# Gated graph network and graph attention, 32 pairs of graphs on one core: the candidate's two products as one operation, the last pair's W product ahead of its softmax, and new leads

## Chip, core and metric

One core of one Trainium2 chip. The metric is the device time of one execution in microseconds, as the median of several runs; the kernel before has 1939.04 us over 3 runs (1937.46 to 1940.88). The profile is of one further execution, whose own time is 1938.19 us.

## What is computed

`x` holds 64 graphs of 256 nodes with 256 features, `adj` their 0/1 edges. All is f32.

```
# layer 0
h = max(layernorm(x), 0)
for i in range(3):
    aggr = A^T (h weight[i])                 # A = (adj != 0)
    gi, gh = aggr w_ih^T + b_ih, h w_hh^T + b_hh
    r, z = sigmoid(i_r + h_r), sigmoid(i_z + h_z)
    n = tanh(i_n + r * h_n)                  # the candidate state
    h = (1 - z) * n + z * h
x = x + h
# layer 1
h = max(layernorm(x), 0);  v = h W^T
e = leaky_relu(v a_left [:, None] + v a_right [None, :])
alpha = softmax(where(adj, e, -1e9))
x = x + alpha v
```

## The kernel before

Graphs go two by two: 32 pairs, and a tile [128, 512] holds one half (`db`) of the features of all 512 nodes of a pair, or for node-major data one graph. TensorE computes in parts: an f32 operand is rounded to f32r (`v0`), and two f16 tiles carry what is left (`v1`) and a copy (`vd`). A product of such operands is one f32r pass (j = 0) and two f16 passes (j = 1, 2) per block of 128 inputs. `split16` (L695) makes the three tiles with two or three instructions of ACT and DVE.

`setup` (L536) turns and splits the weights. It also multiplies `weight[i]` with w_ih^T into one matrix G_i (L657 to L669), so that the aggregate of h itself meets G_i in place of the two products. ACT rounds and copies here (`three`, L644 to L651, `factor`, L600). TensorE starts with 12 transposes of the identity that nobody reads (`fill`, L540, L545); two and five more stand ahead of two later transposes (L546, L626).

`pair(p)` (L812) makes the operations of one pair. Per layer i, `prop` (L862) multiplies h by the adjacency; `split16` splits h (`hs`) and the aggregate (`gs`). Then, per half db of the features, `gate` (L737) makes the products: r with w_hh ahead and with G_i behind, as two operations into one bank ("topT" and "topF"); `nh`, the candidate's product with w_hh (L894), followed by an ACT instruction that adds the bias (L756); `ni`, its product with G_i (L899), in a bank of its own; and z with both (L903). DVE forms (1 + r) * nh (L897), adds ni (L900), ACT takes the tanh (L902) and that of z (L905), and DVE combines (L909 to L913). `passes` (L731) lists the six matmuls of one matrix, and an operation sorts its passes by j:

```python
            seq = [q for m, s in terms for q in passes(bank, cols, m, ts(e, P), s, first)]
            seq.sort(key=lambda q: ((1, 2, 0) if narrow[0] else (0, 1, 2)).index(q[0]))
```

`narrow` tells whether the operation before ended on f16 passes; then this one begins with them and ends on f32r. So each operation changes once between f32r and f16. After the three layers come the residual (L932, L951), the norm, the attention scores, exponentials and two products per graph: `mix` (softmax with h) and `project` (the result with W^T). All pairs but the last turn h and the softmax by DMA (`dma_turn`, L760) and join the halves on ACT (L779).

The last pair has nothing behind it. From its second layer on its two graphs go one by one (`apart`, L853), with 256 columns per matmul, and its attention goes by blocks of 128 rows (L1078 to L1112): exponentials, a transpose by TensorE, a copy, `mix` of 4 products of 128 columns (L1095), a copy (L1102), `project` of 2 products of 256 columns (L1104), the update (L1109) and the store.

The order on each engine is a planner's (`Plan`, L231). `op` notes engine, modelled cost and tiles; `run` (L311) places, again and again, the operation that can start first, ties going to the lower `prio`. That is a due time passed back from its readers, less a lead by name from the table `LEAD` (L28). An operation waits for the earlier operations on its tiles and for a free buffer of its class; there are 8 accumulator banks. `in_turn` (L284) keeps the gate products of one turn (pair and layer, `TURN`, L1117) behind those of the turn before, so that two pairs alternate. Engines run what they get in that order.

Of the kernel before, what the change touches and what calls it, by code (L numbers as in the profile page):

```python
# [25 lines left out]
SWITCH = 16  # L26
SAME = {"PE": 0, "ACT": 115, "DVE": 115, "POOL": 0}
# [3 lines left out]
    "A": -447500, "G 0": 29000, "G 1": -7000, "G 2": 49000, "b_rz": 117000, "b_rz half": -29000, "back 0": -1500,  # L31
    "back 0 gather": 26000, "back 0 of 0": 15000, "back 1": -85000, "back 1 of 0": -54500, "back 1 of 1": 30500,
    "back copy 0": -202500, "back copy 1": 105000, "c0 0": -60000, "c0 1": 76500, "c0 d": -91500, "c1 0": 10500,
    "c1 1": -78500, "c1 d": -12500, "d add 0 of 0": -4000, "d add 1": 65500, "d add 1 of 0": 36500,
    "d add 1 of 1": -5000, "d mul 0": 7500, "d mul 0 of 0": 19500, "d mul 1": 4000, "d mul 1 of 0": 1000,
    "d mul 1 of 1": 44500, "d sub 0": -8500, "d sub 0 of 0": 4000, "d sub 0 of 1": 69000, "d sub 1": 210000,
    "d sub 1 of 0": -169500, "d sub 1 of 1": -32500, "dot 0": -56000, "dot 1": -80000, "exps 0": -5000,
    "exps 0 1": 11500, "exps 1": -24000, "exps 1 0": 500, "fill": 4000, "first A": -28000, "first A16": -2500,
    "first back 0": -8000, "first back 0 gather": -35000, "first back 1": 101500, "first c0 0": -4000,
    "first c0 1": 24500, "first c0 d": 50000, "first c1 0": -8500, "first c1 1": -133500, "first c1 d": 27500,  # L40
    "first d add 0": 5000, "first d add 1": 23000, "first d mul 0": 35500, "first d sub 0": -38000,
    "first d sub 1": 33000, "first dot 0": 4500, "first dot 1": -4000, "first exps 0": 18000, "first exps 1": 41000,
    "first fill": -500, "first g0 0": 39000, "first g0 1": -17000, "first g1 0": 1000, "first g1 1": 8000,
    "first g1 d": -52000, "first h0 0": 8500, "first h0 1": -36500, "first h0 d": 2000, "first h1 0": -30500,
    "first h1 1": 72000, "first h1 d": -8000, "first hi 1": 46000, "first in 0 eps": -36500, "first in 0 pow": -12500,
    "first in 0 relu": 10500, "first in 0 shift": 6000, "first in 0 stats": -60000, "first in 1 eps": -28500,
    "first in 1 pow": -44500, "first in 1 relu": 79000, "first in 1 shift": -19500, "first in 1 stats": -2000,
    "first in hi 0": 125500, "first in hi 1": 39500, "first in lo 0": 51500, "first in lo 1": 500,
    "first leaky 0": 45000, "first leaky 1": -15000, "first line 0": -28500, "first line 1": -46000,
    "first lo 0": -7000, "first lo 1": 13000, "first load": -47500, "first m0 0": 48000, "first m0 1": -10500,  # L50
    "first m0 d": -47500, "first m1 0": 44000, "first m1 1": 72500, "first m1 d": -10000, "first max 0": -13500,
    "first max 1": 8000, "first mid 0 eps": -30500, "first mid 0 pow": 44500, "first mid 0 relu": -33000,
    "first mid 0 shift": -19500, "first mid 0 stats": 20000, "first mid 1 eps": 15000, "first mid 1 pow": 69000,
    "first mid 1 relu": 70500, "first mid 1 shift": -26500, "first mix 0": -50000, "first mix 1": -29000,
    "first nh 0 scale": -20000, "first nh 1 scale": 10000, "first nh 1 topF": 53000, "first ni 0 topF": -6500,
    "first ni 1 topF": -54000, "first out 0": 62000, "first out 1": -500, "first p copy 0": -31500,
    "first p copy 1": -18000, "first p turn 0": -54500, "first p turn 0 gather": 31500, "first p turn 1 gather": 3000,
    "first p0 1": 55000, "first p1 0": -29000, "first p1 1": -16500, "first p1 d": 80500, "first project 0": -22000,
    "first project 1": -7500, "first prop 0": 6000, "first prop 1": -6000, "first r 0": 3000,
    "first r 0 topF": -17000, "first r 1": 51500, "first r 1 topF": 55500, "first r 1 topT": -177500,  # L60
    "first res 0": 47000, "first res 1": -500, "first right 0": -4500, "first right 1": -14000, "first store": 2500,
    "first tanh 0": -59500, "first tanh 1": -3000, "first total": -2000, "first turn 0": -6000, "first turn 1": 40500,
    "first turn copy 0": 500, "first turn copy 1": 44000, "first u 0": 16500, "first u 1": 1500,
    "first u add 0": 16000, "first u add 1": 9500, "first w load full": 4000, "first z 0": -29500,
    "first z 0 topF": -36500, "first z 1 topF": 17500, "g0 0": -9000, "g0 0 of 0": 16000, "g0 0 of 1": -31000,
    "g0 1": -8500, "g0 1 of 0": 16000, "g0 1 of 1": 111000, "g0 d": -25500, "g0 d of 0": 57500, "g0 d of 1": -45500,
    "g1 0": 28000, "g1 0 of 0": -193500, "g1 0 of 1": 1000, "g1 1": 500, "g1 1 of 0": -32000, "g1 1 of 1": 2000,
    "g1 d": 193500, "g1 d of 0": 23500, "g1 d of 1": -5500, "h0 0": -4000, "h0 0 of 0": -115000, "h0 0 of 1": -38000,
    "h0 1": -77000, "h0 1 of 0": -25500, "h0 1 of 1": -12000, "h0 d": -77500, "h0 d of 0": 21500, "h0 d of 1": -28000,
    "h1 0": -72500, "h1 1": -241000, "h1 1 of 0": 87000, "h1 1 of 1": 15500, "h1 d": -212500, "h1 d of 0": -5500,  # L70
    "h1 d of 1": -43000, "hi 0": 23500, "hi 0 of 0": -4000, "hi 0 of 1": 66000, "hi 1": -46000, "hi 1 of 0": -17000,
    "hi 1 of 1": -23000, "ident": -44000, "in 0 eps": 6000, "in 0 pow": -8000, "in 0 shift": -134000,
    "in 0 stats": -10000, "in 1 eps": 4500, "in 1 pow": -8000, "in 1 relu": -2500, "in 1 shift": -307500,
    "in 1 stats": -74500, "in hi 0": -250500, "in hi 1": -91500, "in lo 0": -37500, "last A": 5500, "last A16": 60000,
    "last back 0": 20500, "last back 0 of 0": 4000, "last back 0 of 1": -30000, "last back 1": -99000,
    "last back 1 of 0": -68500, "last d add 0": -33500, "last d add 0 of 0": -154500, "last d add 0 of 1": -33000,
    "last d add 1": 2500, "last d add 1 of 0": 27000, "last d add 1 of 1": -4500, "last d mul 0": -133000,
    "last d mul 0 of 0": -161500, "last d mul 0 of 1": -16000, "last d mul 1 of 0": 5500, "last d mul 1 of 1": -15500,
    "last d sub 0 of 0": -32500, "last d sub 0 of 1": -22500, "last d sub 1": -8000, "last d sub 1 of 0": 24500,
    "last d sub 1 of 1": -125000, "last dot 0": -12000, "last dot 1": 2000, "last exps 0 1": 5000,  # L80
    "last exps 1 0": 10000, "last exps 1 1": 74000, "last fill": 32500, "last g0 0": -97000, "last g0 0 of 0": 97000,
    "last g0 0 of 1": 32000, "last g0 1": 52000, "last g0 1 of 0": 45000, "last g0 1 of 1": -3500,
    "last g0 d": -31000, "last g0 d of 0": -127500, "last g0 d of 1": 5000, "last g1 0": -2000,
    "last g1 0 of 0": -4000, "last g1 1": -11000, "last g1 1 of 0": 102000, "last g1 1 of 1": -18000,
    "last g1 d": 4000, "last g1 d of 0": 161000, "last g1 d of 1": -63500, "last h0 0 of 0": 96000,
    "last h0 0 of 1": 60000, "last h0 1": -66000, "last h0 1 of 0": 35500, "last h0 1 of 1": 19500, "last h0 d": -500,
    "last h0 d of 0": 48000, "last h0 d of 1": -19500, "last h1 0": -1000, "last h1 0 of 0": 37000,
    "last h1 0 of 1": 6500, "last h1 1": 10000, "last h1 1 of 0": 29500, "last h1 1 of 1": 10000, "last h1 d": 20000,
    "last h1 d of 0": 84000, "last h1 d of 1": -10000, "last hi 0": 27500, "last hi 0 of 0": 16000,
    "last hi 0 of 1": -14500, "last hi 1": 4000, "last hi 1 of 0": 33000, "last hi 1 of 1": -2000,  # L90
    "last in 0 eps": 2000, "last in 0 pow": 500, "last in 0 relu": 30000, "last in 0 shift": 57000,
    "last in 0 stats": -18500, "last in 1 eps": 81000, "last in 1 pow": -24000, "last in 1 relu": 16500,
    "last in 1 stats": -32000, "last in hi 0": 81500, "last in hi 1": 16000, "last in lo 0": 15000,
    "last in lo 1": -40500, "last leaky 0": 25000, "last leaky 1": 18000, "last lo 0": 27000,
# [289 lines left out]
def tile_gated_gnn_then_gat(  # L384
# [40 lines left out]
    P = 128  # L425
# [727 lines left out]
```

## Time and profile before

| | |
|---|---|
| median of 3 runs | 1939.04 us |
| profiled execution, own time | 1938.19 us |
| its span | 1936.4 us |
| TensorE busy | 1926.1 us, 10320 matmuls |
| VectorE (DVE) busy | 1647.3 us |
| ScalarE (ACT) busy | 1599.8 us |
| GpSimd (POOL) busy | 197.1 us |
| granted TensorE clock | 1.00 |

The span runs from the first to the last recorded instruction, or the landing of what it stored. A row of the timeline names start and length in us, engine (PE is TensorE, PEld its weight loads), line, operation, written and read tiles, shapes and how many instructions it merges; "f32" with `round` tiles is f32r. In brackets is the engine's idle time before it and what ended it. A matmul's end is modelled, so the distance of two starts tells more than a length. The chain goes back from the last instruction to what released each step.

### The profile page before, as it was taken

The page shows a single profiled execution, that of the slowest core. Times are in us where ns is not written, and L with a number is a line of the kernel's source. Part 1 is how long each engine was busy: PE and PEld are TensorE (multiplying, and loading weights), DVE is VectorE, ACT ScalarE, POOL GpSimd, SP SyncE. Part 2 cuts the span into 40 slices and gives each one's busy share as a digit, 9 for nine tenths or more (in the row PEclk, how much of TensorE's full clock was granted, in tenths as well). Part 3 has the DMA queues.
Part 4 walks back from the last instruction along what each step waited for, and adds up shares of the span by engine and source line. Part 5 has one row for each costly group of instructions (what it writes and reads, how often), then busy time and mean ns, then how long its engine had stood idle before and what let it go on. Part 6 is the DMA issues. An engine that isn't in the chain of part 4 may idle for free.

```text
span 1936.4 us, 31621 instructions
## 1 busy us (share of the span) xinstructions
PE 1926.1 (99%) x10320; PEld 1214.5 (63%) x10320; DVE 1647.3 (85%) x3951; ACT 1599.8 (83%) x2801; POOL 197.1 (10%) x280
## 2 busy tenths in 40 slices
PE   9999999999999999999999999999999999999999
PEld 6556665666666666656666656666566666566667
DVE  7678888888888888889888888888888888888887
ACT  7668888888888888888888888889888888888876
POOL 3001111001011001010010110010110101100000
PEclk9999999999999999999999999999999999999999
DMA  5157786667776777866677877678766777667642
GB/s 142 36 113 125 136 139 126 122 121 151 133 123 119 132 130 141 135 124 119 123 149 132 123 128 124 129 145 136 121 120 124 144 137 122 136 113 128 118 82 61
DMA packets 738119, 240.24 MB, mean 124 GB/s; under 512 B 662160, under 2 KB 737952, under 8 KB 737952
## 3 DMA queue, kind: packets, MB, share of 16 engines
q1 hardware_dynamic: 737920, 238.20, 67.5%
q8 instruction: 81, 1.33, 0.3%
q14 instruction: 86, 0.70, 0.2%
q10 hardware_dynamic: 32, 0.01, 0.0%
HBM read 60.83 MB, written 16.84 MB: 40 GB/s over the span
## 4 chain that ended last, share of the span: by engine, by line
PE 91%; ACT 3%; DMA 2%; DVE 2%; SPq 1%; issue 1%; POOL 0%; ACTq 0%; POOLq 0%
PE bank L734 73%; PE bank L873 8%; PE bank L1056 4%; PE bank L1037 4%; DMA full<-full 2%; SPq L771 1%; ACT full L779 1%; PE bank L664 1%; ACT round L702 0%; ACT half L707 0%; DVE half L704 0%; ACT round L720 0%; DVE small L794 0%; ACT full L807 0%; PE bank L1098 0%
## 5 line engine op out<-in xcount | busy, mean ns | idle before, releaser
L734 PE MATMUL bank<-half,low_hh 128*128 128x512 f16 (+1 forms) x2352 | 613.8, 376 | 0.0
L734 PE MATMUL bank<-half,low 128*128 128x512 f16 (+1 forms) x2352 | 611.7, 375 | 0.1
L734 PE MATMUL bank<-round,fac_hh 128*128 128x512 f32 (+1 forms) x1176 | 411.6, 437 | 0.0
L734 PE MATMUL bank<-round,fac 128*128 128x512 f32 (+1 forms) x1176 | 395.0, 425 | 0.0
L734 PEld LDWEIGHTS <-low 128*128 128x128 f16 x2352 | 216.3, 98 | 267.4 <-issue 45.3
L734 PEld LDWEIGHTS <-low_hh 128*128 128x128 f16 x2352 | 206.2, 98 | 265.3 <-issue 78.9
L779 ACT COPY full<-full 128x1024 uint16<-128x1024 uint16 x306 | 355.7, 1174 | 15.4 <-DMA full<-full 15.2
L734 PEld LDWEIGHTS bank<-round,fac 128*128 128x128 f32 x1176 | 218.6, 189 | 61.5
L734 PEld LDWEIGHTS bank<-round,fac_hh 128*128 128x128 f32 x1176 | 217.1, 189 | 62.7
L801 POOL TENSOR_TENSOR small<-small,nhalf 128x2 f32<-128x2 f32 x128 | 114.5, 902 | 1268.4 <-DVE small L799 1199.3
L704 DVE SCALAR_TENSOR_TENSOR half<-bank,round 128x512 f16<-128x512 f32 (+1 forms) x254 | 171.3, 683 | 48.8 <-ACT half L707 30.8
L756 ACT ACTIVATE bank<-bank,b_nh 128x512 f32<-128x512 f32 (+1 forms) x196 | 127.1, 650 | 96.2 <-PE bank L734 95.9
L905 ACT ACTIVATE full<-bank,b_rz 128x512 f32<-128x512 f32 (+1 forms) x196 | 132.6, 676 | 86.0 <-PE bank L734 85.3
L892 ACT ACTIVATE full<-bank,b_rz 128x512 f32<-128x512 f32 (+1 forms) x196 | 133.8, 683 | 60.4 <-PE bank L734 60.1
L704 DVE SCALAR_TENSOR_TENSOR half<-full,round 128x512 f16<-128x512 f32 (+1 forms) x254 | 170.2, 679 | 8.9 <-ACT round L702 6.1
L702 ACT ACTIVATE round<-bank 128x512 fp32r<-128x512 f32 (+1 forms) x254 | 152.0, 599 | 15.0 <-PE bank L873 11.3
L702 ACT ACTIVATE round<-full 128x512 fp32r<-128x512 f32 (+1 forms) x254 | 155.9, 642 | 6.4 <-DVE full L913 5.2
L721 DVE SCALAR_TENSOR_TENSOR half<-full,round 128x512 f16<-128x512 f32 x184 | 125.9, 686 | 41.1 <-ACT round L720 36.4
L902 ACT ACTIVATE full<-full,vec 128x512 f32<-128x512 f32 (+1 forms) x196 | 140.4, 717 | 24.2 <-DVE full L900 24.2
L911 DVE SCALAR_TENSOR_TENSOR full<-full,full 128x512 f32<-128x512 f32 (+1 forms) x196 | 130.8, 678 | 32.8 <-ACT full L905 32.4
L909 DVE TENSOR_TENSOR full<-full,full 128x512 f32<-128x512 f32 (+1 forms) x196 | 132.8, 678 | 24.6 <-ACT full L902 24.5
L707 ACT ACTIVATE half<-bank 128x512 f16<-128x512 f32 (+1 forms) x254 | 142.6, 601 | 3.7 <-PE bank L873 3.1
(120 smaller groups left out, 2526.2 us busy)
## 6 DMA issues: line engine op xcount, KB each, us to landing
full<-full SPq DMA_DIRECT2D x488, 128.0 KB, 3.5
x<-in_x_dram SPq DMA_DIRECT2D x64, 256.0 KB, 3.2
adj<-in_adj_dram SPq DMA_DIRECT2D x64, 256.0 KB, 3.4
full<-in_x_dram SPq DMA_DIRECT2D x64, 256.0 KB, 3.3
full<-full SPq DMA_DIRECT2D x248, 64.0 KB, 2.5
out_dram<-full SPq DMA_DIRECT2D x62, 256.0 KB, 2.9
full<-line SPq DMA_DIRECT2D x60, 128.0 KB, 4.1
full<-full SPq DMA_TRANSPOSE x306, 3.3
```

What stands on the lines that cost most here:

```text
L702: act(f"{name} 0{of}", cut(A512 if bank else C512), lambda: nc.scalar.activation(v0.t[:, cols], v.t[:, cols], AF.Copy, scale=up), r=[(v, h ...
L704: dve_(f"{name} 1{of}", cut(V512), lambda: nc.vector.scalar_tensor_tensor(v1.t[:, cols], v.t[:, cols], up, v0.t[:, cols].bitcast(F32), op0 ...
L707: act(f"{name} d{of}", cut(A512), lambda: nc.scalar.activation(vd.t[:, cols], v.t[:, cols], AF.Copy, scale=up * unit), r=[(v, has)], w=[(v ...
L734: return [(j, lambda start, j=j, kb=kb: nc.tensor.matmul(bank.t[:, cols], fs(j, kb), s[kb][j].t[:, cols], start=start, stop=True, skip_gro ...
L756: act(name + " scale", fit(575, part), lambda: nc.scalar.activation(bank.t[:, cols], bank.t[:, cols], AF.Identity, bias=bias), r=[("b_nh", ...
L779: act(name, 1065, lambda: nc.scalar.copy(dst.t.bitcast(U16).rearrange("p (j n b) -> p j n b", j=2, b=2), src.t.bitcast(U16).rearrange(f"p ...
L873: nc.tensor.matmul(pa.t[:, ts(g, N)], b, m[:, ts(sb, N)], start=(n == 0), stop=True, skip_group_check=True)
L892: act(f"r {db}{of}", fit(575, part), lambda b=r_, k=pr, db=db, cols=cols: nc.scalar.activation(b.t[:, cols], k.t[:, cols], AF.Tanh, bias=b ...
L902: act(f"tanh {db}{of}", fit(615, part), lambda u=u, en=en, cols=cols: nc.scalar.activation(u.t[:, cols], u.t[:, cols], AF.Tanh, bias=b_i[: ...
L905: act(f"z {db}{of}", fit(575, part), lambda b=z_, k=pz, db=db, cols=cols: nc.scalar.activation(b.t[:, cols], k.t[:, cols], AF.Tanh, bias=b ...
L909: dve2(f"d sub {db}{of}", fit(V512, part), lambda u=u, d=d, cols=cols: nc.vector.tensor_sub(d.t[:, cols], d.t[:, cols], u.t[:, cols]), r=[ ...
L911: dve2(f"d mul {db}{of}", fit(V512, part), lambda d=d, b=z_, cols=cols: nc.vector.scalar_tensor_tensor(d.t[:, cols], b.t[:, cols], 1.0, d. ...
```

## The change

1. `nh` and `ni` become one operation, `new_state`, of 12 matmuls into two banks, sorted by j over both. It replaces the calls at L894 and L899; the ACT and DVE instructions behind them stay. It can start when both the split h and the split aggregate are there, and w_hh and G_i.
2. In the last pair, `h` of each graph is turned by TensorE once its norm is there, copied, multiplied by W^T and copied (`hW`). `mix` is then 2 products of 256 columns per block with `hW`, and its result goes to the update directly. The copy at L1102 and `project` at L1104 go.
3. In `setup`, 11 idle transposes in place of 12 at the start, and in place of the two fixed groups the planner asks for idle transposes in the gaps that it models on TensorE before 12.5 us (all of a gap before 6.5 us, 0.6 of it after, none below one transpose's time). For kb = 1 of w_ih and of `weight[0]` the f16 copy is DVE's in place of ACT's: three instructions.
4. The first loads are modelled at 3200 ns in place of 3900.
5. `LEAD` is replaced: of the names in both tables 4 keep their value.

```diff
+HEAD, COLD, TURN_COLD, TURN_WARM = 12500.0, 6500.0, 213.0, 109.0
...
+            if o.eng == "PE" and self.idle is not None and t < HEAD:
+                gap, slow = t - pe_free, t < COLD
+                if gap > TURN_COLD and pe_free > 0.0:
+                    self.idle(int(gap / TURN_COLD) if slow else int(0.6 * gap / TURN_WARM))
+                s = max(pe_free, t)
+                pe_free = s + (2 * o.occ if slow and o.name != "warm" else o.occ)
...
-        plan.op(name, "SP", 1000, 3900, fn, **kw)
+        plan.op(name, "SP", 1000, 3200, fn, **kw)
...
-        pe("warm", 2500, lambda: fill(12), r=[("ident", ONE)], w=[(idle, ONE)])
-        between = {"0": 2, "1": 5}
+        pe("warm", 2500, warm, r=[("ident", ONE)], w=[(idle, ONE)])
+        plan.idle = fill
...
-            act(f"w d {tag}", 100 + 0.75 * n, lambda: nc.scalar.activation(put(vd), b.t[:, :n], AF.Copy, scale=up), r=[(b, ONE)], w=[(vd, ONE)])
+            if tag in ("ih", 0) and kb == 1:
+                dve(f"w d {tag}", 75 + 1.04 * n, lambda: nc.vector.tensor_scalar(put(vd), b.t[:, :n], up, None, op0=ALU.mult), r=[(b, ONE)], w=[(vd, ONE)])
+            else:
+                act(f"w d {tag}", 100 + 0.75 * n, lambda: nc.scalar.activation(put(vd), b.t[:, :n], AF.Copy, scale=up), r=[(b, ONE)], w=[(vd, ONE)])
...
+    def new_state(name, e, hs, i, gs, tops, bias, part=ALL):
+
+        ph, pn = Buf("bank"), Buf("bank")
+        cols, cost, cost16 = columns(part), PASS if len(part) == 2 else PROP, PASS16 if len(part) == 2 else PROP16
+
+        def go():
+            seq = [(j, bank, run) for bank, m, s in ((ph, "hh", hs), (pn, i, gs)) for j, run in passes(bank, cols, m, ts(e, P), s, True)]
+            started = set()
+            for j, bank, run in sorted(seq, key=lambda q: ((1, 2, 0) if narrow[0] else (0, 1, 2)).index(q[0])):
+                run(bank not in started)
+                started.add(bank)
+
+        tops.append(pe(name + " topF", 4 * (cost + 2 * cost16), go, mixed=True, w=[(ph, ONE), (pn, ONE)],
...
+        act(name + " scale", fit(575, part), lambda: nc.scalar.activation(
+            ph.t[:, cols], ph.t[:, cols], AF.Identity, bias=bias), r=[("b_nh", ONE)], w=[(ph, ONE)])
+        return ph, pn
...
-                    ph = gate(f"nh {db}{of}", en, [("hh", hs)], tops, bias=b_nh[:, db : db + 1], part=part)
+                    ph, pn = new_state(f"nh {db}{of}", en, hs, i, gs, tops, b_nh[:, db : db + 1], part=part)
...
-                    pn = gate(f"ni {db}{of}", en, [(i, gs)], tops, part=part)
...
+        hW = [Buf("full") for _ in range(G)]
+        for g in range(0 if far else G):
...
+            pe(f"h turn {g}", 4 * TR, turn_h, r=[(hb[g], ALL), ("ident", ONE)], w=[(tb, ONE)])
+            act(f"h copy {g}", A512, lambda tb=tb, ht=ht: nc.scalar.copy(ht.t, tb.t), r=[(tb, ONE)], w=[(ht, ONE)])
...
+                        nc.tensor.matmul(pw.t[:, ts(jb, D)], ht.t[:, db * N + jb * P : db * N + (jb + 1) * P], wT[:, db, :],
+                                         start=(db == 0), stop=(db == DB - 1))
+
+            pe(f"hW {g}", 4 * MM, project_rows, r=[(ht, ONE), ("wT", ALL)], w=[(pw, ONE)])
+            act(f"hW copy {g}", A512, lambda pw=pw, b=hW[g]: nc.scalar.copy(b.t, pw.t), r=[(pw, ONE)], w=[(hW[g], ONE)])
...
-            act("mix copy" + name, fit(A512, ONE), lambda ag=ag, pg=pg: nc.scalar.copy(ag.t[:, :N], pg.t[:, :N]), r=[(pg, ONE)], w=[(ag, ONE)])
...
-            pe("project" + name, 2 * MM, project, r=[(ag, ONE), ("wT", ALL)], w=[(pv, ONE)])
+            def mix(g=g, pT=pT, pv=pv):
+                for jb in range(NB):
+                    nc.tensor.matmul(pv.t[:, :D], pT.t[:, ts(jb, P)], parts(hW[g])[:, jb, :], start=(jb == 0), stop=(jb == NB - 1))
+
+            pe("mix" + name, 2 * MM, mix, r=[(pT, ONE), (hW[g], ONE)], w=[(pv, ONE)])
```

## The prediction

> **What bounds the kernel now.** I read the page's busy times and its chain first, then windows of time, then the chain in order of time, and last the timeline of both ends.
>
> ```profile
> span 1936.4 us, 31621 instructions
> ...
> PE 1926.1 (99%) x10320; PEld 1214.5 (63%) x10320; DVE 1647.3 (85%) x3951; ACT 1599.8 (83%) x2801; POOL 197.1 (10%) x280
> ...
> PE 91%; ACT 3%; DMA 2%; DVE 2%; SPq 1%; issue 1%; POOL 0%; ACTq 0%; POOLq 0%
> ```
>
> TensorE is busy in 1926.1 of 1936.4 us and is 91% of the chain. Only 10.3 us can be idle; the next table says where.
>
> ```profile
> 0.00:10.00 10.00, 7.38 (x42) 6.36 (x42) 4.10 (x18) 5.88 (x14) 3.50 (x12) 1.00 0.81 247
> ...
> 400.00:1000.00 600.00, 600.00 (x3191) 375.87 (x3190) 519.83 (x1236) 507.42 (x877) 59.97 (x82) 1.00 0.71 131
> ...
> 1700.00:1800.00 100.00, 97.85 (x521) 60.47 (x519) 86.14 (x207) 81.91 (x142) 9.02 (x12) 1.00 0.66 118
> ...
> 1912.00:1937.00 25.00, 19.82 (x120) 16.46 (x119) 14.40 (x50) 13.34 (x32) 0.95 (x2) 1.00 0.13 44
> ```
>
> Columns are the window, its length, then busy time and count of PE, PEld, DVE, ACT and POOL, then the granted clock. PE idles 2.6 us in the first 10, nothing in the middle, 2.15 in the hundred before 1800, and about 4.6 behind 1912 (the span ends at 1936.4). The chain in order of time repeats with the pair:
>
> ```profile
> 342.06 2.71 PE bank L1037 x24
> ...
> 401.08 2.71 PE bank L1037 x24
> ```
>
> One pair costs 59.02 us, all of it matmuls without a hole. So in the middle only less PE work, or cheaper PE work, shortens the kernel; an earlier DVE or ACT result does nothing there. Elsewhere it is the two ends.
>
> **Merging the candidate state's products** (L894 and L899 become one operation). The matmuls are the same: 6 + 6 before, 12 after. What goes is a change between f32r and f16 passes, which each operation makes once. Price from the 128x512 matmuls of L734, start to start: f16 to f16 is 216 ns, f32 to f32 inside a run 233, f32 to f16 232; from the last f16 to the second f32 it is 451 (216 + 233 would be 449), and the first f16 behind an f32 takes 226. There and back cost 2 + 10 = 12 ns. By whole runs it is less: four f32 in a row cost 945 ns up to the steady f16, six cost 1415; the step is 235 each and leaves 5. The page counts 196 instructions of L756, so 196 operations go and with them 98 changes there and back: 98 times 5 to 12 ns, **0.5 to 1.2 us; I take 0.8**.
>
> The operation now alternates between two accumulators. The row: sixteen f16 matmuls in a row belong to two operations with two banks, and stay at 216 ns with the clock at 1.00. "TensorE: Matmul & The Clock Gate" in the Trainium skill (section "A second HAM failure mode: psum-queue depth-cycling") says that going round the banks can let the clock fall back and forth. It gives no price that I can put in the sum; the row says nothing is lost, and I go by the row.
>
> What the merger takes away is freedom. The h products (L894) need no aggregate and run while ACT and DVE still split it; the candidate's aggregate products (L899) need no w_hh. Three places use that.
>
> In the middle (494 to 497 us) the h products of r and of the candidate lie around the propagation. There the other pair's z products, two operations of 2.7 us, can stand in; ACT and DVE have 15% to spare. I cost it at nothing; if the cover were gone it would be the 1.35 us of one candidate operation per layer, and the period would show it at once.
>
> In the last pair, graphs go apart and cover is thin:
>
> ```profile
> 1906.13 0.60 PE L734 MATMUL bank<-half,low_hh 128*128 128x256 f16 x4
> ...
> 1907.06 0.61 PE L734 MATMUL bank<-half,low_hh 128*128 128x256 f16 x4
> 1907.51 0.38 PE L873 MATMUL bank<-half,half 128*128 128x256 bf16 x2
> ...
> 1908.10 0.48 PE L734 MATMUL bank<-round,fac_hh 128*128 128x256 f32 x2
> ...
> 1909.01 0.48 PE L734 MATMUL bank<-round,fac 128*128 128x256 f32 x2
> 1909.33 1.05 PE L734 MATMUL bank<-half,low 128*128 128x256 f16 x8
> ```
>
> and, in the same timeline, the split that they wait for:
>
> ```profile
> 1908.85 0.42 DVE L704 SCALAR_TENSOR_TENSOR half<-bank,round 128x256 f16<-128x256 f32 x1 [0.36 <-ACT half L707]
> ```
>
> The split of the last aggregate ends on DVE at 1909.27, and the f16 products that read it start at 1909.33: no slack. Until then PE lives on products with w_hh, four operations of six matmuls from 1904.99 on, some 0.68 us each. Two of them (1.36 us) are the candidate's and must now wait. The last propagation (1907.51) needs ACT's rounding of 1905.63, which stood behind the previous pair's exponentials; ordered before them it could run up to 1 us earlier and win back most of this. Bounds 0 and +1.36; **I take +0.7**, the middle. The other such places of the last pair (eight candidate operations in all, 5.4 us) still have the previous pairs' attention products beside them, and I cost them at nothing.
>
> At the start the aggregate half of the candidate fills PE twice (22.72 and 25.60 us, 1.36 us each) before w_hh is ready at about 28.5 us. PE is 100% busy there, with the combined weights G of layers 1 and 2 in hand (four operations of 1.16 us each), which can change places. Nothing, at worst +2.7.
>
> **W^T ahead of the softmax in the last pair.** The tail of the last graph now:
>
> ```profile
> 1929.39 2.05 PE L1098 MATMUL bank<-full,full 128*128 128x128 f32 x16
> ...
> 1930.59 0.37 ACT L1102 COPY full<-bank 128x256 f32<-128x256 f32 x1 [0.81 <-PE bank L1098]
> ...
> 1931.28 1.89 PE L1106 MATMUL bank<-wT,full 128*128 128x256 f32 x8
> 1932.35 0.48 DVE L1109 SCALAR_TENSOR_TENSOR full<-bank,small,full 128x256 f32<-128x256 f32 x1 [3.28 <-PE bank L1106]
> 1933.21 0.48 DVE L1109 SCALAR_TENSOR_TENSOR full<-bank,small,full 128x256 f32<-128x256 f32 x1 [0.38 <-PE bank L1106]
> ```
>
> Sixteen matmuls of the mix, a copy on ACT, eight matmuls with W^T, then the two DVE updates and the store. Afterwards the mix is two products of 256 columns per block, eight instructions of the kind in row L1106, and its result goes to DVE. So those eight start at 1929.39 in place of 1931.28, and all behind them moves by **-1.9 us**. The second block's copy is ready in time (1929.78 against 1930.25).
>
> What is added: for each graph four transposes, a copy, eight matmuls with W^T, a copy. On PE that is 2 x (0.44 + 8 x 0.216) = 4.3, plus the new mixes 16 x 0.216 = 3.5; gone are 32 x 0.112 + 16 x 0.216 = 7.0. PE does 0.75 us more, under a softmax in which it idles (1927.5 to 1928.4 for one). For the last graph: normalised h at 1923.2, then 0.44 + 0.58 + 1.73 + 0.58 with 0.2 behind each, ready at 1927.3, 2 us before 1929.39. ACT gains four copies of 0.58 and loses four of 0.37; it waits 1.6 us before 1927.79. Cost 0, at worst +0.8. No DMA and no store is added; SP's and POOL's queues keep their work, though not its order.
>
> **The start.** Three copies go from ACT to DVE, and idle transposes are put into PE's modelled gaps.
>
> ```profile
> 4.86 0.49 ACT L647 ACTIVATE round<-bank 128x384 fp32r<-128x384 f32 x1 [1.60 <-PE bank L628]
> ...
> 7.51 1.32 ACT L650 ACTIVATE half<-bank 128x384 f16<-128x384 f32 x3
> ```
>
> ACT works almost without pause from 4.86 until the first G products at 9.68; three copies less are 2 x 0.49 + 0.35 = 1.3 us. DVE takes them at some 0.5 each and has 2 us of statistics there that can wait. Bounds 0 and -1.3; **I take -0.6**, since G's f16 passes wait for DVE as well (10.88). An idle transpose costs 109 ns (213 before 6 us), and one too many delays what follows; the gaps hold few, so 0 to +0.5, taken as 0.
>
> Transposes alone had run when they went from 213 to about 110 ns by 6.2 us. "TensorE: Matmul & The Clock Gate" (Part 4) says that transposes don't count as activity for the clock; the row contradicts it. By the page G's first products would run at the slow rate; by the row they run at the full one (384 columns in 163 ns). Fillers stand in both kernels, so the sum is the same by either.
>
> **New leads** reorder every engine's queue. In the middle PE has no hole to win. Before 1850 and behind 200 six PE waits of over 0.25 us add up to about 3.9 us; they may go or come back elsewhere: 0, bounds -3 and +3. In the tail, DVE does other work within the last graph's chain (previous pair's output at 1921.06, which delays L803 by a microsecond; L1109 at 1926.68, 0.4 before the maximum): 0, bounds -1.5 and +1.
>
> **Sum.** -1.9 - 0.8 + 0.7 - 0.6 = **-2.6 us**. The profiled execution took 1938.19 us (span 1936.4 and 1.8 around it), so 1935.6; the median shown is 1939.04, 0.85 above it, and I forecast **1936.4** against that. Measurement tells about 0.2% (3.9 us) from no change: faster is below 1935.2, slower above 1942.9.
>
> **Rivals.**
> 1. Forecast, 1935.0 to 1938.2: chance 0.43. The steady period speaks for it: 1700 us cannot move by more than the changes of pass.
> 2. The new order also closes holes: half the 3.9 us of waits and most of DVE's 1.5 in the tail, another -3.3, so 1933.1 (1930.5 to 1935.1). For it: these waits are idle PE and none is a bound of the work. Against: the trace says nothing of the new order. 0.37.
> 3. The pass changes are worth nothing measurable and new waits eat most of the tail's gain: 1939.3, within 0.2%. 0.09.
> 4. Slower: operations that could run on one input alone are gone, and PE idles at the ends. All eight of the last pair (5.4 us) and both of the start (2.7) are lost: -2.6 - 0.7 + 8.1 = +4.8, 1943.8. It decides once more than 7.2 of these 8.1 us are uncovered, less if waits are added. For it: zero slack at 1909.3. Against: G and attention products lie beside most of them. 0.11.
>
> Low end: case 2 with most of its bounds, 1930.8; high end 1943.0, which leaves out the far half of case 4. Outside lies some 0.15. Faster 0.37 and 0.05 of case 1, so 0.42; slower 0.11; same 0.47.
>
> **What would show it.** Right: pair period 58.99 to 59.02; last store of the tail 1.9 us nearer the last exponentials, with L1098 and L1106 gone; first G products by 9.1 us; a hole of about 0.7 us before the last aggregate's products. Wrong: a period above 59.03 (lost cover in the middle), idle PE of over 2 us between 1860 and 1915, or between 20 and 30; the hW products delaying the last mix beyond the last p copy.

## The result and the profile after

The changed kernel takes **1955.61 us** (median of 5 runs, 1952.32 to 1957.87) against 1939.04 before: ratio 1.0086, 95% interval 1.0075 to 1.0098, **16.6 us slower**, outside the range forecast. The profiled execution took 1955.61 us, so it can be set against the 1938.19 of before: 17.4 us. In the changed kernel the gate matmuls are at L746 (before L734), the propagation at L904 (L873), mix and project at L1067 and L1086 (L1037, L1056), the join copy on ACT at L810 (L779), the gathers ahead of it at L802 (L771), the input loads at L534 (L527). In the experiments whose order is written out, a table shifts the line numbers; the text says which line is which.

The same three lines of the page:

```profile
span 1953.8 us, 31700 instructions
...
PE 1933.9 (99%) x10319; PEld 1225.7 (63%) x10319; DVE 1660.0 (85%) x3954; ACT 1605.7 (82%) x2798; POOL 208.7 (11%) x280
...
PE 69%; DVE 10%; ACT 9%; DMA 7%; issue 3%; SPq 2%; POOL 0%; ACTq 0%; DVEq 0%
```

PE's share of the span is 99% as before, but of the chain it has 69% instead of 91%. DVE, ACT and DMA, 7% together before, have 26%: the end is now handed through them at places all over the kernel. The windows tell where (window, length, PE, PEld, DVE, ACT, POOL, clock, DMA share, GB/s):

```profile
0.00:10.00 10.00, 7.41 (x33) 6.64 (x33) 3.71 (x19) 3.88 (x9) 4.26 (x14) 1.00 0.80 245
10.00:25.00 15.00, 13.60 (x86) 10.91 (x87) 13.13 (x36) 12.03 (x33) 5.20 (x11) 1.00 0.46 153
...
400.00:800.00 400.00, 400.00 (x2128) 251.94 (x2126) 347.14 (x823) 339.07 (x578) 41.37 (x52) 1.00 0.71 128
800.00:1000.00 200.00, 197.19 (x1039) 122.52 (x1037) 172.15 (x408) 168.23 (x294) 22.48 (x28) 1.00 0.76 131
1000.00:1600.00 600.00, 596.33 (x3143) 372.06 (x3142) 517.98 (x1224) 503.50 (x866) 63.66 (x80) 1.00 0.73 128
```

From 800 us on PE stands idle in the middle, where it never did. A busy time hides short waits, since the modelled ends of matmuls overlap, so from here on I count differently: **PE wait** is the distance from each matmul's start to the next one's, less what its shape takes in a steady run (216 ns for 512 f16 columns, 235 for f32r, 110 to 119 for 256, and so on). By stretch, in us, with the PE work (the sum of those steady times) beside it:

| kernel | work | 0-60 | 60-400 | 400-1700 | 1700-1880 | 1880-end |
|---|---|---|---|---|---|---|
| before | 1914.65 | 4.41 | 2.35 | 3.06 | 3.77 | 3.20 |
| after | 1916.23 | 9.08 | 6.10 | 13.05 | 4.03 | 0.39 |
| difference | +1.58 | +4.67 | +3.75 | +9.99 | +0.26 | -2.81 |

The prediction read 10.3 us of idle time in before from the busy time; by this count it is 16.8. The differences sum to 17.4, the whole loss. Ten of it arise between 400 and 1700 us, in few places. PE's waits in 600 to 1700 us (before, this view has no row at all):

```profile
PE bank L1086 <- DVE half L716: 4.6, 3, 2.1
PE bank L904 <- DVE half L733: 1.7, 6, 0.5
```

Columns are the sum, how often, and the longest. Three waits of project (L1086) for a half tile of DVE make 4.6 us. The chain in order of time through the longest shows where such a wait begins:

```profile
828.23 7.25 DMA full<-full
...
835.55 1.17 ACT full L810
836.72 0.02 issue
836.75 0.43 DVE half L722
...
844.45 0.61 DVE half L716
845.06 0.05 issue
845.11 0.94 PE bank L1086 x7
```

The last gather DMA took 7.25 us to land; the join copy stood at the head of ACT's queue for it (the join of an earlier gather of the same group had already waited 3.20 us, to 831.13); DVE then worked through what had piled up; its half tile reached PE late. ACT's waits for DMA ahead of joins, after and then before:

```profile
ACT full L810 <- DMA full<-full: 51.9, 45, 3.6
```

```profile
ACT full L779 <- DMA full<-full: 15.2, 16, 4.0
```

And the reason, from SP's timeline at that place:

```profile
822.55 0.57 SPq L534 DMA_DIRECT2D x<-in_x_dram  x1
823.18 0.98 SPq L534 DMA_DIRECT2D adj<-in_adj_dram  x2
824.25 4.82 SPq L802 DMA_DIRECT2D full<-full  x6
```

Three loads of 256 KB, for a pair that needs them some 40 us later, are issued directly ahead of the six DMAs of three gathers that ACT waits for. In the order of before most gathers come first, and two of these loads stand ahead of the two DMAs of one gather:

```profile
1045.73 6.72 SPq L771 DMA_DIRECT2D full<-full  x10
1052.49 0.61 SPq L527 DMA_DIRECT2D x<-in_x_dram  x1
...
1054.52 1.11 SPq L527 DMA_DIRECT2D adj<-in_adj_dram  x2
1057.76 1.30 SPq L771 DMA_DIRECT2D full<-full  x2
```

This became **theory B**: the new leads put loads ahead of gathers, in an order that places the joins just where the gathers land. **Theory A**, which I held first, was the lost cover: operations that can run on h alone are gone.

### The profile page after: what moved, and what is told of

It reads as the page before. It is cut to its first block, busy times and chain, and to the rows that moved or that the text cites. A ratio compares the mean times of both kernels' runs of the same rounds, so it can differ in the third digit from the quotient of the medians.

```text
span 1953.8 us, 31700 instructions
## 1 busy us (share of the span) xinstructions
PE 1933.9 (99%) x10319; PEld 1225.7 (63%) x10319; DVE 1660.0 (85%) x3954; ACT 1605.7 (82%) x2798; POOL 208.7 (11%) x280
## 4 chain that ended last, share of the span: by engine, by line
PE 69%; DVE 10%; ACT 9%; DMA 7%; issue 3%; SPq 2%; POOL 0%; ACTq 0%; DVEq 0%
PE bank L746 55%; PE bank L904 7%; DMA full<-full 6%; PE bank L1086 3%; PE bank L1067 3%; ACT full L810 2%; DVE half L716 2%; ACT round L714 1%; SPq L802 1%; ACT full L838 1%; DVE small L825 1%; DVE full L941 1%; ACT half L719 1%; DVE full L943 1%; DVE half L733 1%
## 5 line engine op out<-in xcount | busy, mean ns | idle before, releaser
L746 PE MATMUL bank<-half,low_hh 128*128 128x512 f16 (+1 forms) x2352 | 652.6, 376 | 0.4 <-DVE half L716 0.4
L746 PE MATMUL bank<-half,low 128*128 128x512 f16 (+1 forms) x2352 | 649.5, 375 | 0.0
L746 PE MATMUL bank<-round,fac_hh 128*128 128x512 f32 (+1 forms) x1176 | 418.8, 441 | 0.0
L810 ACT COPY full<-full 128x1024 uint16<-128x1024 uint16 x306 | 357.8, 1171 | 57.5 <-DMA full<-full 51.9
L746 PEld LDWEIGHTS <-low 128*128 128x128 f16 x2352 | 223.2, 98 | 268.8 <-issue 23.7
L746 PE MATMUL bank<-round,fac 128*128 128x512 f32 (+1 forms) x1176 | 374.8, 407 | 0.0
L746 PEld LDWEIGHTS <-low_hh 128*128 128x128 f16 x2352 | 207.8, 98 | 254.5 <-issue 74.1
L832 POOL TENSOR_TENSOR small<-small,nhalf 128x2 f32<-128x2 f32 x128 | 126.9, 991 | 1665.0 <-DVE small L830 1664.9
L746 PEld LDWEIGHTS bank<-round,fac 128*128 128x128 f32 x1176 | 219.6, 188 | 57.8
L746 PEld LDWEIGHTS bank<-round,fac_hh 128*128 128x128 f32 x1176 | 214.4, 189 | 59.2
L928 DVE SCALAR_TENSOR_TENSOR full<-full,bank 128x512 f32<-128x512 f32 (+1 forms) x196 | 131.8, 673 | 42.2 <-ACT bank L787 19.9
L719 ACT ACTIVATE half<-bank 128x512 f16<-128x512 f32 (+1 forms) x254 | 151.3, 598 | 8.6 <-PE bank L904 6.8
```

The lines of the kernel that those rows point to most:

```text
L719: act(f"{name} d{of}", cut(A512), lambda: nc.scalar.activation(vd.t[:, cols], v.t[:, cols], AF.Copy, scale=up * unit), r=[(v, has)], w=[(v ...
L746: return [(j, lambda start, j=j, kb=kb: nc.tensor.matmul(bank.t[:, cols], fs(j, kb), s[kb][j].t[:, cols], start=start, stop=True, skip_gro ...
L810: act(name, 1065, lambda: nc.scalar.copy(dst.t.bitcast(U16).rearrange("p (j n b) -> p j n b", j=2, b=2), src.t.bitcast(U16).rearrange(f"p ...
L928: dve(f"u {db}{of}", fit(S512, part), lambda u=u, k=ph, b=r_, cols=cols: nc.vector.scalar_tensor_tensor(u.t[:, cols], b.t[:, cols], 1.0, k ...
```

## The experiments

Times are medians; ratios are against the kernel before in the same job (1937.83, 1938.45, 1938.35 and 1938.08 us in the four jobs).

**Parts alone, planner run anew.** merge_alone is before with `new_state` and the old leads; tail_alone is before with hW; split_again is after with `nh` and `ni` apart again, `ni` with the lead of `nh`; head_undone is after with the setup of before and its leads for setup and pair 0.

```diff
 merge_alone
-                    ph = gate(f"nh {db}{of}", en, [("hh", hs)], ...)
+                    ph, pn = new_state(f"nh {db}{of}", en, hs, i, gs, ...)
-                    pn = gate(f"ni {db}{of}", en, [(i, gs)], ...)
 split_again: the reverse, in the changed kernel
 tail_alone
+            pe(f"hW {g}", 4 * MM, project_rows, ...)
-            pe("project" + name, 2 * MM, project, ...)
```

> The kernel before with the merged candidate operation alone; tail, start and lead table are those of before (the leads of the ni products fall away with them). Theory A (the merger itself takes the w_hh products from ahead of the propagation, the layer loop loses its slack of 0.6 us and more, and DMA variation reaches TensorE): the period of an undisturbed pair is 58.98 us, but TensorE waits between 60 and 1850 us add up to over 6 us in place of some 4, and the median is 1943 or more. Theory B (the merger is harmless, the new lead table alone makes the order tight): middle waits stay at 3 to 5 us and the median is 1937 to 1940.

> The kernel before with the last pair's W product ahead of its softmax alone, leads of before (new names have lead 0). Both theories: the middle is as before. If the tail is worth what the prediction said, the last store comes 1.9 us nearer the last exponentials and the median is 1936.5 to 1938; if the added transposes, products and copies stand in the way of the last graph's chain, 1938.5 to 1941.

> The changed kernel with the candidate's products as two operations again; each takes the lead that the merged one has in the new table. Theory A: the loop gets its slack back, middle waits (60 to 1850 us) fall from about 14 us to 4 or less, and the median is 1943 to 1947, the start still being late by some 5 us. Theory B: the new table keeps the order tight, middle waits stay over 9 us and the median is 1951 to 1957. Against both: leads made for other operations can make an order that is bad in a third way.

> The changed kernel with the start of before: fixed idle transposes, three copies on ACT, first loads modelled at 3900 ns, and the leads of before for the setup and for pair 0. Everything else is as changed. If the start costs 4.7 us (waits before 25 us of 9.0 against 4.3), the first G product is back at about 9.7 us in place of 16.5, and the median falls by 4 to 6 us to 1949.5 to 1951.5. If the start's lateness is hidden behind later waits, the median stays within 1.5 us of 1955.6.

Measured: merge_alone 2057.0 us, ratio 1.0611 (1.0595 to 1.0627); split_again 2071.8, 1.0697 (1.0669 to 1.0726); head_undone 2100.2, 1.0837 (1.0819 to 1.0855). PE waits 136 to 177 us, in every pair; split_again and head_undone missed their forecasts by over 100 us. None of these tells a part's price: here each lead table fitted one set of operations, and with another the planner made a different, bad order for the whole kernel. So in the later kernels the order is written out. tail_alone kept its order up to the last pair, so it does tell: 1938.55 us, ratio 1.0001 (0.9992 to 1.001), no gain. Its ACT in the tail:

```profile
1926.21 0.48 ACT L997 ACTIVATE full<-bank,small 128x256 f32<-128x256 f32 x1
1926.58 0.59 ACT L1089 COPY full<-bank 128x512 f32<-128x512 f32 x1
1927.04 0.50 ACT L997 ACTIVATE full<-bank,small 128x256 f32<-128x256 f32 x1
1929.64 0.51 ACT L1104 ACTIVATE full<-full,small 128x256 f32<-128x256 f32 x1 [2.10 <-DVE small L1002]
```

From these exponentials (1929.64) to the end of the span are 7.1 us, 8.6 before (from 1927.79): 1.5 of the 1.9 us forecast are there. But the copy of the turned h (L1089) stands between the two leaky-relu rows ahead of the softmax, and the exponentials begin 1.85 us later than before, of which the later gate products explain 0.7 (end at 1915.26 against 1914.54). On TensorE the balance is small: its waits from 1880 us on fall from 3.20 to 2.01 us, and its work rises by 0.81.

**The order written out.** In the next kernels each engine's order is a table, and only what is named moves. hh_ahead: after, operation cut in two, the first `nh` of each layer of pairs 1 to 30 directly behind the last gate product of the turn before. split_in_place: cut in two, side by side. merge_in_place: before, with `nh` merged into `ni` at the later place for pairs 1 to 26. start_of_before: after, with setup and the first 40 us of the plan as before.

```diff
 hh_ahead         PE: z 1 (turn before), +nh 0, prop 0, prop 1, r, ..., -nh 0, ni 0
 split_in_place   PE: -[nh 0 + ni 0]  +nh 0, ni 0
 merge_in_place   PE: -nh 0, prop 0, prop 1, r, -ni 0  +[nh 0 + ni 0]
 start_of_before  all engines: operations planned before 40 us in the order of before
```

> The changed kernel with its order on every engine written out and kept, but the candidate's products are two operations again, and of pairs 1 to 30 the w_hh product of the first half (nh 0) stands right behind the last gate product of the turn before, ahead of the propagation: 90 operations of six matmuls, 1.35 us each, move; all others stay. Theory A (the merger took cover from ahead of the propagation, so that late DMA landings and the ACT queue behind them reach TensorE): waits between 100 and 1850 us fall from 13.9 us to 5 or less, and the median is 1945 to 1949. Theory B (the order of ACT, DVE and DMA under the new leads is tight by itself, whoever stands ahead of the propagation): waits stay over 9 us, median 1951 to 1957.

> The changed kernel's order kept, each candidate operation cut in two that stand side by side where the one stood. Nothing can run earlier than before, but 196 operations more change between f32r and f16. The price of the changes alone: the undisturbed pair goes from 58.985 to about 59.02 us, 1.2 us in all, so the median is 1955.5 to 1958; if the changes are free, within 0.5 us of the changed kernel's 1955.6.

> The kernel before with its order kept on every engine; for pairs 1 to 26 the two candidate operations become one that stands where the later of them (ni) stood, with the bias and the first DVE step behind it moved only as far as they must be. Theory A: the propagation now stands 1.35 us or more earlier against inputs that are as late as before, of which the second half had 0.57 us to spare, and TensorE waits in every pair: 1 to 3 us a pair, 26 to 80 us in all, median 1965 to 2015. Theory B (the merger costs no cover in the middle): period 58.98 to 59.1 us and median 1936 to 1940.

> The changed kernel, but what the planner of the kernel before placed in the first 40 us of its plan (setup and the first pair's first layer, with the old fillers and the three copies on ACT) stands first on each engine in the old order, with the candidate's products merged where the later one stood; the rest follows in the changed kernel's order. If the start costs 4.7 us, waits before 25 us fall from 9.0 to about 4.3 and the median is 1950 to 1952.5. If what is late at the start is absorbed by later waits, or the seam costs as much, it stays within 2 us of 1955.6.

Measured: hh_ahead 1962.4 us, 1.0122 (1.0105 to 1.0139), above both forecasts. Cover for the propagation is back, and the time is worse. Its propagation (L1286) hardly waits; project (L1469) does:

```profile
PE bank L1469 <- DVE half L1098: 10.0, 11, 1.7
...
PE bank L1286 <- DVE half L1115: 1.9, 2, 1.3
```

So theory A in this form fell. split_in_place: 1954.4, 1.0079 (1.0064 to 1.0094), below both forecasts and not to be told from after. merge_in_place: 1979.4, 1.0211 (1.0195 to 1.0226), 41 us slower than before at unchanged PE work. The chain repeats at

```profile
416.86 1.36 PE bank L1457 x12
...
477.36 1.36 PE bank L1457 x12
...
537.86 1.36 PE bank L1457 x12
```

every 60.50 us instead of 59.03, while the joins wait only 6.7 us for DMA. So in the old order the merger costs about 1.5 us of cover per pair. The order of the new leads has that cover (an undisturbed pair takes 58.99 us there), and it has what theory B names; that one needs the other is not shown, and the next kernels speak against it. start_of_before: 1952.0, 1.0067 (1.0052 to 1.0082), some 3.7 us better than after by the ratios, though the intervals overlap. In its profile PE's waits before 25 us fall from 9.0 to 5.5 us (forecast: 4.3), but 3.4 us arise between 25 and 60 us, where one order hands over to the other. So the waits of the start go, and nearly as much comes back at the handover.

**The loads on SP.** loads_behind is after with the loads of pairs 3 to 27 behind the three gathers. loads_and_start adds the start of before. light_loads keeps the order and thins the bytes: it leaves out seven eighths of these loads and of the stores, and so computes other numbers. old_loads_ahead does the reverse to before.

```diff
 loads_behind     SP: -load x, load adj, load adj
                      gather back 1, gather back 0, gather p turn 1
                     +load x, load adj, load adj
 old_loads_ahead  SP: +load x, load adj, load adj
                      gather back 0, gather turn 1, gather turn 1, back 1
                     -load x, load adj, load adj
 light_loads      -dma_start(parts(b), rows(src, g))
                  +dma_start(parts(b)[:16], rows(src, g)[:16])
```

> The changed kernel with its order of all instructions written out, and one thing moved on SP: in pairs 3 to 27 the three input loads of 256 KB (one of x, two of adj) that stood directly ahead of three gathers (back 1, back 0, p turn 1) go directly behind them. Nothing else moves. Theory B (the new leads put these loads ahead of the gathers, the gathers land late, an ACT join waits for them at the head of its in-order queue, DVE follows, and TensorE waits for a DVE half): the gathers of this place land in 3 to 4 us instead of 5 to 7, the waits of the join copies for DMA fall from 52 us to under 30, the waits of TensorE between 100 and 1850 us lose some 10 of their 23 us, and the time is 1943 to 1949. Rival A (the cover lost with the merger, whatever the DMA does): the join waits may fall, TensorE waits as before, time 1952 to 1958.

> The kernel loads_behind and, besides, the first 40 us of the plan in the order of before (setup code of before without the idle turns). If the two causes are separate, their gains add: 3 to 4 us below loads_behind, so 1940 to 1946 by theory B, 1949 to 1953 by rival A. Below 1938 it would beat the kernel before.

> The changed kernel, same instructions in the same order, but for pairs 4 to 27 the loads of x and adj and the stores of the output move 16 of their 128 partitions (an eighth of the bytes; this leaves out part of the input and of the output, so the numbers computed are others). Theory B: the gathers no longer share the queue with these bytes, the join copies wait under 25 us for DMA, and the time is as low as loads_behind or lower, 1941 to 1948. Rival A: 1952 to 1958.

> The kernel before with its order written out, and in pairs 4 to 27 its three loads (one of x, two of adj) moved on SP ahead of a gather of back 0 and two gathers of turn 1, so that gathers land behind loads as they do in the changed kernel. Theory B holds both halves needed, late gathers and an order without slack: here TensorE has 0.6 to 3.6 us of slack behind the DVE limbs, so the join waits rise from 15 us towards 30, TensorE's waits by 0 to 5 us, time 1938 to 1944. If late gathers alone were enough, the time would rise by some 10 us to 1948 or more.

Measured, with the PE waits of 400 to 1700 us and the joins' waits for DMA:

| kernel | us | ratio to before | PE wait | joins wait |
|---|---|---|---|---|
| after | 1955.61 | 1.0086 (1.0075 to 1.0098) | 13.05 | 51.9 |
| loads_behind | 1945.9 | 1.0038 (1.0023 to 1.0053) | 3.49 | 10.9 |
| light_loads | 1944.4 | 1.0033 (1.0020 to 1.0046) | 2.19 | 17.0 |
| loads_and_start | 1939.95 | 1.0009 (0.9999 to 1.0019) | 2.66 | 9.3 |
| before | 1938.35 | | 3.06 | 15.2 |
| old_loads_ahead | 1943.6 | 1.0033 (1.0019 to 1.0046) | 8.00 | 82.0 |

Theory B's times hold for three of the four; loads_and_start lies 0.05 us under its range, and its gain over loads_behind is 6.0 us where 3 to 4 was forecast. The joins of old_loads_ahead wait 82 us where some 30 was forecast. Rival A's times (1952 to 1958, and 1949 to 1953) fail in all three kernels for which it gave one. SP, the joins and the chain of loads_behind (its joins are at L1184, gathers at L1176, loads at L908):

```profile
822.47 6.13 SPq L1176 DMA_DIRECT2D full<-full  x6
828.66 0.63 SPq L908 DMA_DIRECT2D x<-in_x_dram  x1
829.33 0.99 SPq L908 DMA_DIRECT2D adj<-in_adj_dram  x2
```

```profile
ACT full L1184 <- DMA full<-full: 10.9, 17, 1.7
```

```profile
PE 89%; ACT 3%; DMA 3%; DVE 3%; issue 1%; SPq 1%; POOL 0%; ACTq 0%; DVEq 0%
```

The six gather DMAs of this place, as far as the trace tells their landing, in after (issued from 824.25 us on) and in loads_behind (from 822.47 on):

```profile
DMA to landing us min/median/max: 5.7/6.1/7.1
```

```profile
DMA to landing us min/median/max: 3.6/4.4/5.2
```

In light_loads they take 3.5 to 4.3 us, 3.6 in the median. In loads_behind three loads per pair, in 25 pairs, moved behind three gathers, and nothing moved on another engine: the gathers land earlier, the joins wait a fifth, PE is back at 89% of the chain, and 9.7 of 16.6 us are gone. With the start of before as well another 6.0 go (1945.9 to 1939.95). The profiles place only 2.3 of these at the start: waits before 60 us fall from 9.2 to 7.7 (before 25 us from 9.1 to 4.6, with 3.1 new at the handover), and PE has 0.8 less work. 4.5 lie between 1700 and 1880 us (5.4 against 0.9), where the two kernels have the same order; quiet_merged below, with that order too, waits 3.4 there. So where the rest of the 6.0 comes from is not shown. old_loads_ahead shows the other half of the cause (join L1164; the halves of ACT and DVE that project, L1441 there, waits for):

```profile
ACT full L1164 <- DMA full<-full: 82.0, 53, 3.7
```

```profile
PE bank L1441 <- ACT half L1092: 3.0, 3, 1.4
PE bank L1441 <- DVE half L1089: 2.4, 3, 1.6
```

Its joins wait even longer than after's, 82 us, yet PE loses 4.9 us in 400 to 1700 us instead of 10: the order of before has more slack between a join and PE. The loss of after took both, late gathers and a tight order.

**What the parts are worth once nothing waits.**

```diff
 quiet_merged     loads_and_start; SP, pair 2: both loads of adj behind gather p turn 1
 quiet_split      quiet_merged; PE: -[nh + ni]  +nh, ni
 quiet_merged_50  quiet_merged; 50 us of the order of before instead of 40
```

> The kernel loads_and_start with one more move on SP: in pair 2 the two loads of adj that stand ahead of a gather of p turn 1 go behind it. In loads_and_start (1939.95 us) a join of pair 3 still waited for a late gather and TensorE waited 2.25 us at 184 us and 1.27 us at 199 us. Theory B: these two waits go or shrink below 1 us together, time 1936.5 to 1938.5, level with the kernel before or up to 0.1% faster. If they come from the order of ACT and DVE by itself: unchanged, 1939 to 1941.

> The kernel quiet_merged with each merged operation cut in two that stand side by side, in the same order otherwise, so that the product with w_hh and the one with G change between f32r and f16 passes on their own. This prices what the merger itself saves where nothing waits: 0.04 us per layer and half that the pair period showed, so 1.0 to 1.5 us slower than quiet_merged in the time TensorE is busy; near the limit of what the rounds can tell. Rival: cutting also gives back cover (the half that is ready first can start), then it is as fast or faster than quiet_merged.

> The kernel quiet_merged with the first 50 us instead of the first 40 us of the plan in the order of before. The waits at the handover between the two orders (4 us between 25 and 60 us in loads_and_start) move with it; if they belong to the handover and not to the start, the time changes by under 2 us either way, 1935 to 1940.

Measured: quiet_merged 1939.6, 1.0012 (1.0003 to 1.002); quiet_split 1941.4, 1.0018 (1.0009 to 1.0026); quiet_merged_50 1940.2, 1.0011 (1.0002 to 1.002). The first forecast failed (the profiled execution of quiet_merged is also its slowest, 1942.4): the waits of pair 3 shrank at two places (2.25 to 1.27, 1.27 unchanged) and 1.3 us arose at 176 us; 60 to 400 us hold 5.15 us of PE waits, as in loads_and_start (5.53) and against 2.35 before. The third moved nothing and lies 0.2 us over its range. So the 3 us between 60 and 400 us stay open; every kernel with the new order there has them (5.15 to 7.7 us against 2.35 before), and that is all I can say. quiet_split is 1.8 us slower by medians, but the intervals overlap, and its profile has 2.5 us more of waits between 60 and 400 us, so this is no price of the changes of pass. The distance of a matmul to the same one of the next pair (median over 400 to 1640 us) tells more: 58.987 merged, 58.993 split, 59.027 before.

No version beats the kernel before; loads_and_start can't be told from it.

## Why the prediction was wrong

**The step that failed: "New leads reorder every engine's queue. In the middle PE has no hole to win"**, costed 0 with bounds -3 and +3. I looked at what PE could win and never at what SP's queue could lose. I wrote that "SP's and POOL's queues keep their work, though not its order" and let that cost nothing; the order was the cost. From 60 to 1880 us PE's waits grew by 14.0 us where this term had 0, at most 3. Moving three loads behind three gathers gives 9.7 us back.

**The start**, -0.6 forecast, was +5.4 (4.67 of waits, 0.77 of PE work, idle turns included). I priced three copies that move from ACT to DVE; the leads also reorder the first loads. The first G products were to come by 9.1 us; they come at 16.52. The loads of weight, W and x now stand ahead of w_ih, and PE turns weight and W first; how much each of the two costs no run separates:

```profile
0.74 0.96 SPq L534 DMA_DIRECT2D x<-in_x_dram  x2
1.75 0.46 SPq L582 DMA_DIRECT2D full<-in_L_gnn_weight_dram  x1
2.25 0.47 SPq L582 DMA_DIRECT2D full<-in_L_gnn_W_dram  x1
2.77 0.98 SPq L582 DMA_DIRECT2D full<-in_L_gnn_w_ih_dram  x2
```

```profile
6.27 1.11 PE L638 MATMUL bank<-ident,full 128*128 128x128 f32 x4 [1.24 <-DMA full<-in_L_gnn_weight_dram]
...
16.52 0.60 PE L676 MATMUL bank<-round,round 128*128 128x384 f32 x2
```

PE's first useful transposes run at 6.27 instead of 3.98. With the start of before (in loads_and_start) the first G products are back at 9.55. The median falls by 3.6 to 6.0 us then, of which the profiles show 0.9 to 2.3 in the first 60 us; the handover between the orders may hide the rest of the start's own price.

**The change of passes**, -0.8: the pair period did fall as forecast, to 58.99:

```profile
358.53 8.01 PE bank L746 x36
...
417.52 8.01 PE bank L746 x36
```

but for another reason. Cutting the operations again returns 0.006 of the 0.040 us per pair: the 98 changes there and back that go are worth some 0.2 us in the whole kernel, below my 0.5. The rest of the 0.040 belongs to the order, in a way that no run shows. That the period met the forecast was luck.

**Cover in the middle**, "I cost it at nothing": half right. The other pair's products can stand in, as the period shows, but only in a new order of everything; in the old one it is 1.5 us per pair, about a third of the 1.35 per layer (4.05 per pair) that I gave for lost cover. The price of re-arranging was not in my sum.

**The alternating banks**: the clock is 1.00 in every window above and the period is the shortest measured, so going round two accumulators cost nothing here; the section "A second HAM failure mode: psum-queue depth-cycling" of "TensorE: Matmul & The Clock Gate" in the Trainium skill describes a clock that goes back and forth when a kernel cycles through its banks; nothing of it shows here, as the row in the prediction had said.

**The last pair's hole**, +0.7: none appeared (0.39 us of waits from 1880 us to the end). **The tail**, -1.9 at cost 0: by the balance -2.0 (waits -2.81, work +0.81), but not in the way forecast. From the last exponentials (1946.40) to the end are 7.4 us against 8.6, so 1.2 shorter and not 1.9, and PE does not idle under the softmax any more; it is busy without a hole to the last mix:

```profile
1944.84 1.03 PE L1149 MATMUL bank<-full,full 128*128 128x256 f32 x4
1945.71 1.89 PE L1124 MATMUL bank<-wT,full 128*128 128x256 f32 x8
1947.43 0.38 PE L1142 MATMUL bank<-ident,full 128*128 128x128 f32 x2
1947.65 1.03 PE L1149 MATMUL bank<-full,full 128*128 128x256 f32 x4
1948.52 0.38 PE L1142 MATMUL bank<-ident,full 128*128 128x128 f32 x2
1948.74 1.89 PE L1149 MATMUL bank<-full,full 128*128 128x256 f32 x8
```

The added products fill the idle time that was to hide them. With the old order (tail_alone) the gain was nil, so that the -2.0 met the forecast is the new order's doing, and luck.

Of the rivals, case 4 had the sign right and the mechanism wrong: it put the loss on lost cover at both ends, from 1860 us on, where PE now waits less. No rival had a DMA in it.

## To carry to other kernels

When a change rewrites the order of all queues, price the transfer queue first: ask which transfers stand ahead of one that an in-order engine waits for, and how much slack lies between that engine and the bound; a load that is needed 40 us later has no place in front of a gather that is needed now. A part's price could not be had here by undoing it and letting the planner choose anew (6 to 8% slower in three cases of four); write the order out and move one thing. And a busy share of 99% says little: the share of the chain (91 to 69%) and the waits by stretch told the story.

## What the hardware showed unexpectedly

The landing of a gather of 128 KB depended on what was issued just ahead: at the place shown a median of 6.1 us with three loads of 256 KB ahead, 4.4 with the loads behind, and 3.6 with the loads ahead but an eighth of their bytes; over the whole kernel 3.9 after and 3.5 before. Late landings held ACT's joins for 3.2 us and then 0.33 (to 835.55), and reached PE 10 us later (845.1), through DVE's queue, as a wait of 2.0 us. And a change between f32r and f16 passes was nearly free: about 1 ns for each of the six that go per pair (0.006 us over six operations), where single distances of starts had suggested 12 there and back.
